# A two-layer transformer kernel: the order inside one step of layer 1's attention loop

## The chip, the core and the metric

The kernel runs on one core of a Trainium2 chip, in one launch. The metric is the device time of that core in microseconds, from the start of the execution to its end. A core has five engines that each work through a queue of their own, in order, and wait for one another by semaphores: TensorE (PE, matrix products and transposes), VectorE (DVE), ScalarE (ACT), GpSimd (POOL) and SyncE (SP, which issues DMAs here).

## The reference

The input `x` holds 2 sequences of 2048 tokens with 512 features (4096 tokens), the context 2 times 128 tokens. Four blocks follow one another, each added to `x`. All of it is float32.

```python
x = x + L0_xattn(layernorm(x), ctx, ...)   # 16 heads of 64, rope, tanh cap, causal
x = x + L0_ffn(layernorm(x), ...)          # fake-quantised gate, up, down; inner width 1408
x = x + L1_xattn(layernorm(x), ctx, ...)   # 16 heads of 32, masked
x = x + L1_ffn(layernorm(x), ...)          # one of 8 experts by argmax

def L1_xattn(q, k, v, mask, ...):
    Q = split_heads(q @ Wq.T + bq);  K = ...;  V = ...
    scores = where(mask, 1e-9, Q @ K.T / sqrt(32))
    return (softmax(scores) @ V) @ Wo.T + bo

def L1_ffn(x, Wg, bg, We, be):
    probs = softmax(x @ Wg + bg)              # 512 logits a token
    idx, p = argmax(probs), max(probs)
    return relu(x @ We[idx % 8] + be[idx % 8]) * p
```

## The kernel before

Tokens are worked on in 32 tiles of 128 tokens (`NT` = 32); `xs[n]` is the running `x` of tile `n` and stays on the chip. Layer 0's attention and feed-forward come first and take up to some 929 us of the span. Then comes the loop that the change is in, `for n in range(NT)`, whose step `n` does the attention of tile `n` and, behind it by one and two tiles, the rest of layer 1 for tiles `n - 1` and `n - 2`. Experts follow.

From that loop on the order of PE, DVE, ACT and POOL is the order in which the program is written, with no scheduler between (`manual_schedule`). So each engine's queue in a step is what the calls below issue, one after another:

- `biased(n - 1)`: POOL adds the output's bias to `xs[n - 1]` (L949).
- `normed(m)`: variance and reciprocal root for a tile five ahead (L92 to L101). The function that it returns centers that tile (DVE, `xn1`, L821) and, from tile 6 on, starts its transpose by DMA. In the steps 2 to 26 there is one such tile; these returned functions are the list `firsts`.
- `scores(n)`: 32 small products on PE into `sc` (L892). Then DVE masks half of the heads (L900) and takes their maxima (L905), and the other half likewise.
- `exponentials(n)`: 16 activations on ACT (L914); those of the second half leave their sums too.
- `queries(blk + 1, fs)`: the queries of the next block of 256 tokens. A step makes two of the four feature groups, one by `fs[:1]` and one by `fs[1:]`, each with 4 products on PE (8 instructions of 256 columns, L872) and an activation that puts the result into `qT` (L875).
- `shares(n, half)`: DVE takes the reciprocal of the half's sums (L922), POOL multiplies the half's 128x1024 exponentials by it (L923). For half 0 DVE has also to take the sums (L920).
- `logits(n - 2)`: PE, 4 products of 512 columns (L978) into `pl`. `picked(n - 2)`: DVE's largest logit and its index (L984, L988). `gated(n - 2)`: an activation over `pl` (L996) and small DVE instructions.
- `projected(n - 1)`: PE, the attention's output times `Wo` (L955) into `pw`, and the residual: DVE adds `pw` to `xs[n - 1]` (L956).
- `normed2(n - 1)`: statistics of the new `xs[n - 1]` (L92, L94, L963, L100), POOL's reciprocal root (L101). The function that it returns centers the tile (DVE, `xn2`, L821).
- `turned(n)`: PE transposes the shares, four tiles `pt` of four transposes each (L116); ACT copies each back (L931). The first two `pt` are of half 0, the others of half 1.
- `turned2(n - 1)`: PE transposes `xn2` (L116), ACT copies it (L972).
- `mixed(n)`: PE multiplies shares and values into `po` (L941), ACT copies that to `oT` (L946).

All of PE's results but the scores go through a pool `psm` of four banks. Both centerings come from one function, whose two wide operands, the tile and the scale spread over its columns, lie in SBUF:

```python
def center_by(dst, x, mean, r):
    nc.vector.scalar_tensor_tensor(dst, x, mean, r.to_broadcast([P, D]), ALU.subtract, ALU.mult)
```

The steps 24 to 29 carry a first part of the experts' routing on DVE as well; the steps 30 and 31 have no queries, but an expert each.

Of the kernel before, what the change touches and what calls it, by code (L numbers as in the profile page):

```python
# [18 lines left out]
AF = mybir.ActivationFunctionType  # L19
ALU = mybir.AluOpType  # L20
# [4 lines left out]
P = 128  # L25
B, S, T, D = 2, 2048, 128, 512
ND = D // P
NT = B * S // P
# [5 lines left out]
H1, DH1 = 16, 32  # L34
# [29 lines left out]
def two_layers(ctx: ExitStack, tc: tile.TileContext, a, out):  # L64
    nc = tc.nc
# [85 lines left out]
    with ExitStack() as l0:  # L151
# [231 lines left out]
        def queries(u, par):  # L383

            k, g = divmod(u, NG)
            j, b = blocks[k]
            if par == 0:
                if j not in tabs:
                    tables_in(j)
                ropes[u] = [mid.tile([P, B0], F32, name=f"rt{i}", bufs=1) for i in range(4)]  # L390
            pq, rt = psm.tile([P, B0], F32, name="pq", tag="m"), ropes[u]
            for c in range(ND):
                nc.tensor.matmul(  # L393
                    pq, wqs[c // 2][:, c % 2, par, g * P : (g + 1) * P], xnTs[k][:, c, :], start=(c == 0), stop=(c == ND - 1)
                )
            cos, sin = tabs[j]
            if par == 0:
                nc.vector.tensor_tensor(rt[0], pq, cos, ALU.mult)  # L398
                nc.vector.tensor_tensor(rt[1], pq, sin, ALU.mult)
                return  # L400
            qs[u] = [mid.tile([P, B0], F32, name=f"q{i}") for i in range(2)]
            nc.vector.tensor_tensor(rt[2], pq, sin, ALU.mult)  # L402
            nc.gpsimd.tensor_tensor(qs[u][0], rt[0], rt[2], ALU.subtract)  # L403
            nc.vector.tensor_tensor(rt[3], pq, cos, ALU.mult)
            nc.gpsimd.tensor_tensor(qs[u][1], rt[3], rt[1], ALU.add)
# [38 lines left out]
        def projected(u, t):  # L444

            k, g = divmod(u, NG)
            if g == 0:
                pws[k, t] = psq.tile([P, D], F32, name="pw", tag="pw", bufs=NB0)
            pw = pws[k, t]
            for f in range(2):  # L450
                nc.tensor.matmul(  # L451
                    pw, atts[u][:, f, t * P : (t + 1) * P], wo[:, 2 * g + f, :],
                    start=(g == 0 and f == 0), stop=(g == NG - 1 and f == 1),
                )
# [182 lines left out]
    with ExitStack() as up:  # L637
# [137 lines left out]
        rest = values(0)  # L775
# [86 lines left out]
        else:  # L862
            nc.scalar.copy(dst, transposed(psm, xn1s[n]))

    def queries(blk, fs):

        if blk not in qTs:
            qTs[blk] = mid.tile([P, ND, B1], F32, name="qT1")
        for f in fs:
            pq = psm.tile([P, B1], F32, name="pq", tag="m")  # L870
            for c in range(ND):
                nc.tensor.matmul(  # L872
                    pq, wq1[:, c, f * P : (f + 1) * P], xTs[blk][:, c, :], start=(c == 0), stop=(c == ND - 1)
                )
            nc.scalar.activation(  # L875
                qTs[blk][:, f, :], pq, AF.Identity, bias=bq[:, f : f + 1], scale=1.0 / math.sqrt(DH1)
            )

    def kept_keys(n):

# [35 lines left out]
    def shares(n, half):  # L916

        s, sm = ss_[n][half][0], sums[n][:, 8 * half : 8 * half + 8]
        if half == 0:
            nc.vector.tensor_reduce(sm, s, AX.X, ALU.add)  # L920
        rs = small.tile([P, 8], F32, name="rs")
        nc.vector.reciprocal(rs, sm)  # L922
        nc.gpsimd.tensor_tensor(s, s, rs.unsqueeze(2).to_broadcast([P, 8, T]), ALU.mult)  # L923
# [27 lines left out]
    def projected(n):  # L951

        pw = psm.tile([P, D], F32, name="pw1", tag="m")
        for c in range(ND):
            nc.tensor.matmul(pw, os_[n][:, c, :], wo1[:, c, :], start=(c == 0), stop=(c == ND - 1))  # L955
        nc.vector.tensor_tensor(xs[n], xs[n], pw, ALU.add)  # L956

    xn2, xn2T, pls, picks = {}, {}, {}, {}

    def normed2(n):  # L960

        mv = variance(xs[n])
        nc.vector.tensor_copy(xw[n][:, D : D + 1], mv[:, 0:1])  # L963
        r = xw[n][:, D + 1 : D + 2]
        rsqrt_eps(r, mv[:, 1:2])
        xn2[n] = mid.tile([P, D], F32, name="xn2", bufs=1)
        return lambda: center_by(xn2[n], xs[n], mv[:, 0:1], r)
# [6 lines left out]
    def logits(n):  # L974

        pl = pls[n] = psm.tile([P, D], F32, name="pl", tag="m")
        for c in range(ND):
            nc.tensor.matmul(pl, xn2T[n][:, c, :], wgate[:, c, :], start=(c == 0), stop=(c == ND - 1))  # L978
# [12 lines left out]
    def gated(n):  # L991

        negm, i8 = picks[n]
        pe = small.tile([P, 1], F32, name="pe1")

        nc.scalar.activation(  # L996
            scs[min(n + 2, NT - 1)][:, 0].rearrange("p c k -> p (c k)"), pls[n], AF.Exp, bias=negm, accum_out=pe
        )
        ei = small.tile([P, 1], U32, name="ei")
        nc.vector.tensor_scalar(ei, i8[:, 0:1], NE - 1, None, ALU.bitwise_and)  # L1000
        ef = small.tile([P, 1], F32, name="ef")
        nc.vector.tensor_copy(ef, ei)
        nc.vector.tensor_scalar(hot[:, n, :], iota_e, ef, None, ALU.is_equal)
        nc.gpsimd.tensor_tensor(cum[:, n + 1, :], cum[:, n, :], hot[:, n, :], ALU.add)
        nc.vector.memset(xw[n][:, D + 3 : D + 4], 0.0)

        def rest():
            nc.vector.reciprocal(xw[n][:, D + 2 : D + 3], pe)
            nc.sync.dma_start(out=x_dram[n * P : (n + 1) * P, :], in_=xw[n])

        return rest
# [224 lines left out]
    for n in range(NT):  # L1236
        blk, t = n // NB1, n % NB1
        ahead = blk + 1 < nblk
        fs = range(t * ND // NB1, (t + 1) * ND // NB1)
        if n > 0:  # L1240
            biased(n - 1)
        firsts = [m for m in (n + 2 * NB1, n + 2 * NB1 + 1) if m < NT and (m >= TURNED) == (m > n + 2 * NB1)]
        firsts = [normed(m) for m in firsts]
        scores(n)
        if 4 <= n < 4 + 2 * NE and n % 2 == 0:

            nc.scalar.dma_start(out=rowadd, in_=v_dram[(n - 4) // 2].partition_broadcast(P))

        late = t == 0 and n > 1
        if ahead and not late:  # L1250
            queries(blk + 1, fs[:1])
        if late:
            logits(n - 2)
        exponentials(n)
        if ahead and late:
            queries(blk + 1, fs[:1])
        if n == 0:
            for i in range(NT - held, NT - held + 2):
                down(i)
                widened(i + 2)  # L1260
        shares(n, 0)
        if n > 1:
            if not late:
                logits(n - 2)
            picked(n - 2)
        shares(n, 1)
        if n > 0:
            projected(n - 1)
            normed2(n - 1)()
        firsts = [first() for first in firsts]  # L1270
        rest = gated(n - 2) if n > 1 else None
        if n + 1 < NT:
            kept_keys(n + 1)
        for first in firsts:
            if first:
                first()
        if 0 < n <= NE:
            load(we[:, n - 1], a["L1_ffn_We"][n - 1].rearrange("(c p) f -> p c f", p=P))
        if ahead:
            queries(blk + 1, fs[1:])  # L1280
        if n == 0:
            for i in range(NT - held + 2, NT):
                down(i)
            dwn.close()
            ffd.close()
            moe = ctx.enter_context(tc.tile_pool(name="moe", bufs=1, side="right"))
            we = moe.tile([P, NE, ND, D], F32, name="we")
        if 4 <= n < 4 + 2 * NE:
            e, half = divmod(n - 4, 2)
            for c in range(2 * half, 2 * half + 2):  # L1290
                nc.gpsimd.tensor_tensor(we[:, e, c, :], we[:, e, c, :], rowadd, ALU.add)
        if not ahead:

            expert(n - NT + NB1)
        turned(n)
        if rest:
            rest()
        if n > 0:
            turned2(n - 1)
        mixed(n)  # L1300
        if t == NB1 - 1 and blk + 2 < nblk:
            for t in range(NB1):
                turned1((blk + 2) * NB1 + t)
        if n == NTA + 2:
            route = routing(True)
        if route:
            for _ in range({NTA + 2: 4, NTA + 3: 1}.get(n, 2)):
                if next(route, route) is route:
                    route = None
                    for j in range(4):  # L1310
                        gathered(j)
                    break
        if n == NT - NB1 - 1:
            for j in range(3):
                centered_x(j)
            turned_x2(0)
    biased(NT - 1)
    projected(NT - 1)
    normed2(NT - 1)()
    logits(NT - 2)  # L1320
    picked(NT - 2)
# [54 lines left out]
```

## Time and profile before

| | |
|---|---|
| median of 3 runs | 1600.61 us (1597.93 to 1601.00) |
| profiled execution: its time, its span | 1599.43 us, 1597.4 us |
| TensorE clock granted, mean | 0.995 |
| busy: PE, DVE, ACT, POOL | 1551.3, 1192.5, 720.4, 586.8 us |
| loop: first scores of step 0, of step 31 | 928.9, 1416.1 us |
| a step between 2 and 23 | 15.32 us (337.1 us for 22) |

The span runs from the first to the last instruction; the execution's own time is 2.0 us more. PE's busy time is the sum of its instructions' times, which overlap their neighbours'. In the timeline a row is one instruction or several equal ones: start, time, engine, line, operation, and in brackets how long the engine had sat idle and what released it. Where PE's rows are concerned, an instruction's end is modelled, and the next may start before it.

### The profile page before, as it was taken

What the parts mean: (1) busy time and instruction counts of PE and PEld (TensorE: products, weight loads), DVE (VectorE), ACT (ScalarE), POOL (GpSimd) and SP (SyncE); (2) the same over time, 40 slices, a digit from 0 to 9 for tenths busy, and PEclk for the clock granted to TensorE, in tenths of its full rate; (3) what the DMA queues carried; (4) which work ended last, traced back from release to release, by engine and by line L of the source; (5) the groups of instructions that cost most, each with busy time, mean ns of one, the idle gap of its engine ahead of it and who ended that gap; (6) DMA issues with size and microseconds to landing.
All of it is one profiled execution on the core that took longest, in us unless ns stands there. A gap on an engine that the chain in (4) does not pass through costs nothing. (4 is left out here: it accounts for less than half of the span.)

```text
span 1597.4 us, 26167 instructions
## 1 busy us (share of the span) xinstructions
PE 1551.3 (97%) x9542; PEld 909.1 (57%) x9542; DVE 1192.5 (75%) x2333; ACT 720.4 (45%) x1537; POOL 586.8 (37%) x580
## 2 busy tenths in 40 slices
PE   7999999999999999999999999999999999999997
PEld 5655555555555555544444466666666666654443
DVE  3467777777777886589986678888888888877442
ACT  1222222222222222243335566777777776763442
POOL 2232222222222222110005654555565444544553
PEclk9999999999999999999999999999999999999999
DMA  9511212111111220367768734221311111114553
GB/s 321 188 37 41 47 40 47 40 47 40 51 46 41 59 60 1 117 169 205 179 173 278 271 132 143 48 47 34 55 45 36 41 28 41 41 47 131 162 162 89
DMA packets 180571, 150.90 MB, mean 94 GB/s; under 512 B 97089, under 2 KB 144665, under 8 KB 180444
## 3 DMA queue, kind: packets, MB, share of 16 engines
q1 hardware_dynamic: 170188, 127.25, 28.5%
q0 software_dynamic: 6240, 18.70, 3.8%
q10 hardware_dynamic: 4016, 3.29, 0.9%
q8 instruction: 76, 1.25, 0.3%
q14 instruction: 51, 0.42, 0.1%
HBM read 89.97 MB, written 41.79 MB: 82 GB/s over the span
## 5 line engine op out<-in xcount | busy, mean ns | idle before, releaser
L419 ACT ACTIVATE pr<-sc 128x1024 f32<-128x1024 f32 x64 | 65.6, 1024 | 421.6 <-PE sc L414 421.4
L393 PE MATMUL pq<-xnT,wq 128*128 128x256 f32 x1024 | 254.4, 391 | 0.0
L451 PE MATMUL pw<-wo,att 128*128 128x512 f32 x512 | 230.8, 593 | 0.0
L393 PEld LDWEIGHTS pq<-xnT,wq 128*128 128x128 f32 x1024 | 184.4, 189 | 67.1 <-issue 44.0
L914 ACT ACTIVATE s<-s,mx 128x128 f32<-128x128 f32 x512 | 175.3, 388 | 28.1 <-DVE mx L905 28.1
L923 POOL TENSOR_TENSOR s<-s,rs 128x1024 f32<-128x1024 f32 x64 | 120.9, 1903 | 149.6 <-DVE rs L922 149.1
L403 POOL TENSOR_TENSOR q<-rt,rt 128x256 f32<-128x256 f32 x64 | 46.7, 730 | 339.7 <-DVE rt L402 335.2
L451 PEld LDWEIGHTS pw<-wo,att 128*128 128x128 f32 x512 | 96.9, 190 | 96.4 <-issue 89.9
L441 DVE RECIPROCAL rd<-sc 128x256 f32<-128x256 f32 x64 | 112.4, 1757 | 46.5 <-PE sc L435 46.5
L1195 PE MATMUL pz<-we,x 128*128 x312 | 139.3, 598 | 1.8 <-ACT x L832 1.6
L872 PE MATMUL pq<-xT,wq 128*128 128x256 f32 x512 | 122.6, 382 | 0.0
L978 PE MATMUL pl<-wgate,xnT 128*128 128x512 f32 x256 | 116.7, 599 | 0.0
L955 PE MATMUL pw<-wo,oT 128*128 128x512 f32 x256 | 115.2, 592 | 0.7 <-ACT oT L946 0.7
L872 PEld LDWEIGHTS pq<-xT,wq 128*128 128x128 f32 x512 | 96.0, 190 | 33.1 <-issue 20.3
L398 DVE TENSOR_TENSOR rt<-pq,rope_cos 128x256 f32<-128x256 f32 x64 | 27.0, 422 | 104.2 <-PE pq L393 104.2
L749 ACT ACTIVATE gate<-pg,gsc 128x512 f32<-128x512 f32 x88 | 60.5, 687 | 93.9 <-PE pg L744 84.0
L1195 PEld LDWEIGHTS pz<-we,x 128*128 128x128 f32 x312 | 58.2, 192 | 68.4 <-issue 65.2
L92 DVE BATCH_NORM_STATS2 st<-x 128x6 f32<-128x512 f32 x130 | 89.4, 688 | 6.0 <-DMA x<-in_ctx 3.8
L744 PE MATMUL pu<-xqT,wuT 128*128 128x512 bf16 x352 | 90.3, 379 | 2.6 <-DVE h L752 2.4
L744 PE MATMUL pg<-xqT,wgT 128*128 128x512 bf16 x352 | 90.3, 379 | 0.0
L900 DVE SCALAR_TENSOR_TENSOR s<-sc,keep 128x1024 f32<-128x1024 f32 x64 | 78.1, 1220 | 14.3 <-PE sc L892 9.1
L955 PEld LDWEIGHTS pw<-wo,oT 128*128 128x128 f32 x256 | 48.6, 190 | 55.3 <-issue 53.6
(226 smaller groups left out, 2811.8 us busy)
## 6 DMA issues: line engine op xcount, KB each, us to landing
h_dram<-h SPq DMA_DIRECT2D x88, 256.0 KB
hq<-h_dram SPq DMA_DIRECT2D x31, 704.0 KB
x_dram<-x SPq DMA_DIRECT2D x32, 258.0 KB
x<-in_x SPq DMA_DIRECT2D x32, 256.0 KB
we<-in_L_ffn_We SPq DMA_DIRECT2D x8, 1024.0 KB
xnT<-in_x_turned SPq DMA_DIRECT2D x14, 512.0 KB
along<-stat_dram SPq DMA_DIRECT2D x14, 256.0 KB
w_in<-in_L_ffn_w_gate SPq DMA_DIRECT2D x11, 256.0 KB
```

What stands on the lines that cost most here:

```text
L92: nc.vector.bn_stats(out=st, in_=x)
L393: nc.tensor.matmul(pq, wqs[c // 2][:, c % 2, par, g * P : (g + 1) * P], xnTs[k][:, c, :], start=(c == 0), stop=(c == ND - 1))
L441: nc.vector.reciprocal(rd, sc[:, 0, B0:])
L451: nc.tensor.matmul(pw, atts[u][:, f, t * P : (t + 1) * P], wo[:, 2 * g + f, :], start=(g == 0 and f == 0), stop=(g == NG - 1 and f == 1),)
L744: nc.tensor.matmul(dst, w[:, c, i * P : (i + 1) * P], xqTs[blk][:, c, :], start=(c == 0), stop=(c == ND - 1),)
L872: nc.tensor.matmul(pq, wq1[:, c, f * P : (f + 1) * P], xTs[blk][:, c, :], start=(c == 0), stop=(c == ND - 1))
L900: nc.vector.scalar_tensor_tensor(s, sc[:, 2 * half : 2 * half + 2].rearrange("p r c k -> p (r c) k"), -MASKED, keeps[n].unsqueeze(1).to_br ...
L914: nc.scalar.activation(s[:, h, :], s[:, h, :], AF.Exp, bias=mx[:, h : h + 1], **accum)
L923: nc.gpsimd.tensor_tensor(s, s, rs.unsqueeze(2).to_broadcast([P, 8, T]), ALU.mult)
L955: nc.tensor.matmul(pw, os_[n][:, c, :], wo1[:, c, :], start=(c == 0), stop=(c == ND - 1))
L978: nc.tensor.matmul(pl, xn2T[n][:, c, :], wgate[:, c, :], start=(c == 0), stop=(c == ND - 1))
L1195: nc.tensor.matmul(pz, ring[j][:, c, :], we[:, bass.ds(e, 1), c, :], start=(c == 0), stop=(c == ND - 1))
```

## The change

All of it is in the order within a step. On PE the projection of tile `n - 1` now comes first behind the scores, then the logits of tile `n - 2`, then the first group of queries, and of the second group three of its four products; the fourth comes behind the transposes of the shares. Before, the first group of queries stood ahead of the logits in odd steps and behind them in even ones, and the projection behind both.

On DVE the residual's addition now stands between the two halves of the shares, ahead of `picked`; the reciprocal of half 1 follows these. The centering of the tile five ahead (`xn1`) now stands ahead of the centering of tile `n - 1` (`xn2`); it stood behind it.

On ACT the activation of the first group of queries comes behind the exponentials in all steps, and that of the second group behind the four copies of the shares. The queues of POOL and SP keep their order.

```diff
-    def queries(blk, fs):
+    def queries(blk, fs, held=0):
...
+            products(range(ND - held))
+            if held:
+                return lambda: products(range(ND - held, ND)), rest
+            rest()
...
-        nc.vector.tensor_tensor(xs[n], xs[n], pw, ALU.add)
+        return lambda: nc.vector.tensor_tensor(xs[n], xs[n], pw, ALU.add)
...
-        late = t == 0 and n > 1
-        if ahead and not late:
-            queries(blk + 1, fs[:1])
-        if late:
+        residual = projected(n - 1) if n > 0 else None
+        if n > 1:
             logits(n - 2)
         exponentials(n)
-        if ahead and late:
+        if ahead:
             queries(blk + 1, fs[:1])
...
         shares(n, 0)
+        if residual:
+            residual()
         if n > 1:
-            if not late:
-                logits(n - 2)
             picked(n - 2)
         shares(n, 1)
-        if n > 0:
-            projected(n - 1)
-            normed2(n - 1)()
+        second = normed2(n - 1) if n > 0 else None
+
         firsts = [first() for first in firsts]
+        if second:
+            second()
         rest = gated(n - 2) if n > 1 else None
...
-        if ahead:
-            queries(blk + 1, fs[1:])
+
+        end = queries(blk + 1, fs[1:], 1) if ahead else ()
...
         turned(n)
+        for part_ in end:
+            part_()
         if rest:
             rest()
         if n > 0:
             turned2(n - 1)
         mixed(n)
...
-    projected(NT - 1)
+    projected(NT - 1)()
```

Built, a step has four banks for these tiles in turn: `pw`, `pl` and the two `pq`. The second `pq` keeps its bank over the transposes, so the four `pt` take the banks of `pw`, of the first `pq`, of `pl`, and then again that of the first `pt`.

More of the change, by code (lines that the diff above doesn't have):

```diff
@@ L870, in queries, with products, rest @@
             pq = psm.tile([P, B1], F32, name="pq", tag="m")
-            for c in range(ND):
-                nc.tensor.matmul(
-                    pq, wq1[:, c, f * P : (f + 1) * P], xTs[blk][:, c, :], start=(c == 0), stop=(c == ND - 1)
-                )
-            nc.scalar.activation(
-                qTs[blk][:, f, :], pq, AF.Identity, bias=bq[:, f : f + 1], scale=1.0 / math.sqrt(DH1)
-            )
+            def products(cs, f=f, pq=pq):
+                for c in cs:
+                    nc.tensor.matmul(
+                        pq, wq1[:, c, f * P : (f + 1) * P], xTs[blk][:, c, :], start=(c == 0), stop=(c == ND - 1)
+                    )
+            def rest(f=f, pq=pq):
+                nc.scalar.activation(
+                    qTs[blk][:, f, :], pq, AF.Identity, bias=bq[:, f : f + 1], scale=1.0 / math.sqrt(DH1)
+                )
+            products(range(ND - held))
+            if held:
+                return lambda: products(range(ND - held, ND)), rest
+            rest()
     def kept_keys(n):
```

## The prediction

> **What bounds the kernel now.** First the page's busy times: PE is busy nearly throughout, so only PE's waits can be won.
>
> ```profile
> PE 1551.3 (97%) x9542; PEld 909.1 (57%) x9542; DVE 1192.5 (75%) x2333; ACT 720.4 (45%) x1537; POOL 586.8 (37%) x580
> ```
>
> Next, busy times by stretch, for steps 2 to 23: 337.1 us, 15.32 us each.
>
> ```profile
> 965.30:1302.40 337.10, 335.02 (x2557) 223.26 (x2556) 289.45 (x614) 252.88 (x769) 185.42 (x163) 1.00 0.21 47
> ```
>
> Then the timeline of one step; its scores start at 1072.51. Below, every time counts from there.
>
> ```profile
> 1080.15 0.20 DVE L922 RECIPROCAL rs<-sums 128x8 f32<-128x8 f32 x1
> 1080.27 0.65 DVE L984 MAX8 m<-pl 128x8 f32<-128x512 f32 x1
> 1080.52 3.76 POOL L923 TENSOR_TENSOR s<-s,rs 128x1024 f32<-128x1024 f32 x2 [3.77 <-DVE rs L922]
> 1081.09 0.69 DVE L988 FIND_INDEX8 i<-m,pl 128x8 uint32<-128x512 f32 x1
> 1082.01 0.20 DVE L922 RECIPROCAL rs<-sums 128x8 f32<-128x8 f32 x1 [0.23 <-ACT s L914]
> 1082.31 1.89 PE L872 MATMUL pq<-xT,wq 128*128 128x256 f32 x8
> 1082.59 0.69 DVE L956 TENSOR_TENSOR x<-x,pw 128x512 f32<-128x512 f32 x1 [0.37 <-PE pw L955]
> 1083.31 0.70 DVE L92 BATCH_NORM_STATS2 st<-x 128x6 f32<-128x512 f32 x1
> 1084.04 1.91 PE L116 MATMUL pt<-ident,s 128*128 128x128 f32 x16
> 1084.33 0.14 DVE L100 TENSOR_SCALAR ve<-mv 128x1 f32<-128x1 f32 x1
> 1084.55 0.55 POOL L101 TENSOR_TENSOR x<-ve,minus_half 128x1 f32<-128x1 f32 x1 [0.27 <-DVE ve L100]
> 1085.13 0.75 DVE L821 SCALAR_TENSOR_TENSOR xn<-x,mv 128x512 f32<-128x512 f32 x1 [0.66 <-POOL x L101]
> 1085.80 0.74 DVE L821 SCALAR_TENSOR_TENSOR xn<-x,mv,r 128x512 f32<-128x512 f32 x1
> 1086.03 0.63 PE L116 MATMUL pt<-ident,xn 128*128 128x128 f32 x4
> 1086.59 1.31 PE L941 MATMUL po<-s,v 128*32 128x128 f32 x32
> 1087.83 1.17 PE L892 MATMUL sc<-kT,qT 32*128 32x128 f32 x32
> ```
>
> PE transposes the shares from 11.53; sixteen at 0.11 us let it go on at 13.28. The transposes of xn2 start at 13.52, 0.15 after their centering ends (13.37): PE loses about 0.24 a step there, all that a better order can win. The other chain ends near it: POOL's two multiplications run back to back, 1.90 each, from 8.01 to 11.77, and PE wants half 1 at 12.40. That is 0.63 of slack.
>
> Last, the timeline where DVE meets POOL, in steps 1 and 0 and just before the loop:
>
> ```profile
> 959.25 1.27 POOL L949 TENSOR_TENSOR x<-x,bob 128x512 f32<-128x512 f32 x1
> 959.32 1.75 DVE L821 SCALAR_TENSOR_TENSOR xn<-x,mv 128x512 f32<-128x512 f32 x1 [0.85 <-POOL x L101]
> ```
>
> ```profile
> 939.97 4.10 POOL L923 TENSOR_TENSOR s<-s,rs 128x1024 f32<-128x1024 f32 x2 [0.45 <-ACT qT L875]
> 940.37 1.92 DVE L882 TENSOR_SCALAR keep<-masks 128x128 f32<-128x128 uint8 x1
> ```
>
> ```profile
> 925.03 0.88 DVE L804 CAST hb<-hi 128x1408 bf16<-128x1408 int8 x1
> 925.19 1.13 POOL L101 TENSOR_TENSOR r<-ve,minus_half 128x1 f32<-128x1 f32 x1 [0.23 <-DVE ve L100]
> ```
>
> A centering takes 0.75; issued under POOL's addition it took 1.75 and ended 0.55 after it (961.07 against 960.52). The mask took 1.92 under L923, 0.22 elsewhere. POOL's root takes 0.55; under a DVE cast it took 1.13 and ended 0.41 after it. So these instructions shut each other out.
>
> **The change part by part, in a step from 2 to 23.** *Scores to the first reciprocal:* unchanged, so half 0's stands at 7.64. *Projection first:* it needs oT, which ACT copies from 0.11 to 0.70 (1072.62, 0.59 long); the scores hold PE until 1.1. Nothing is paid; 0.4 covers it, and a later oT would cost its excess. *Residual sooner:* pw is ready by 5, so DVE adds behind the reciprocal: 7.76 (0.12 later, as MAX8 is now). That lengthens DVE's queue ahead of half 1 by 0.72 (1082.59 to 1083.31): MAX8 8.48, index 9.30 (0.82 later), the reciprocal 10.02. Today it waits for ACT until 9.50, so 0.52 of the 0.72 shows. POOL starts 0.37 after a reciprocal: half 1 runs 10.39 to 12.29, not 11.77.
>
> *PE up to half 1:* the same products in another order, less a quarter of the second queries (a quarter of 1.73 is 0.43): transposes start at 11.10, and half 1 is wanted at 11.97. It comes at 12.34 (in step 1 PE started 0.05 after POOL's end: 958.78, 958.83). A new wait of 0.37. Behind it stand PE's eight transposes (0.9) and the held product (0.43): PE is free for xn2 at about 13.70. The held product fills the old 0.24 hole, but later than the hole was.
>
> *The centering of the tile ahead, now first:* statistics follow the reciprocal, ve at 11.16 (10.14 plus 1.02, as 1083.31 to 1084.33), so this centering is issued at about 11.3, in the middle of POOL's half 1. Today both centerings run while POOL is idle. By the row of step 1 it ends 0.55 after POOL: 12.84. POOL's root for xn2, queued behind half 1, meets that centering as the row before the loop met the cast: done 0.41 after it, 13.25. xn2 then runs 13.28 to 14.03, and PE's transposes start 0.15 later, 14.18: another wait of 0.48. From there 0.56 to po and 1.24 to the next scores, as now: 15.98. The step grows by 0.66; 22 of them by **14.5**.
>
> The Trainium skill speaks to this ("SBUF — State Buffer", Who interferes with whom): a DVE instruction with two SBUF inputs and a GpSimd instruction that reads SBUF lock each other out, and the second to issue waits for the first's end. Taken to the letter the centering would run whole after POOL (13.04), the root whole after that, and the step would grow by 1.0, 22 of them by 22, as an estimate. The rows above have durations (0.55 and 0.41 instead of 0.75 and 0.55), so I take 0.66.
>
> *ACT and banks:* the first queries' activation now follows the exponentials: pq ends near 9.9, so it runs to 10.4, the gating to 11.1; the transposes that need those banks start at 11.5 and 12.34. The fourth pt reuses the first's bank: copied by 12.3, wanted at 12.8. The second activation, behind the copies, ends by 14.6; the next scores need it after 16. All nothing; the least cover is 0.5.
>
> *The other steps.* Step 0: PE waits for half 1 anyway, so the held product adds its 0.43: 0.4. Step 1 has two tiles to center ahead of xn2, and POOL's bias addition can lock out xn2 in turn: between a gain of 0.9 (no lock) and a loss of 1.5; by the row at 959.32 xn2 ends some 0.6 later than now, so 0.7. Steps 24 to 29: step 24's growth is swallowed, since step 25's scores wait for routing on DVE; the end of 25 moves by 1.0 (0.52 and the lock's 0.46), 26 adds 0.3, 27 to 29 have no tile ahead and add 0.2 each: 1.9, between 0.5 and 4. Steps 30 and 31: transposes stand at 11.95 behind the expert, xn2 comes 0.05 late: 0.1. The tail keeps its order.
>
> Sum: 0.4 + 0.7 + 14.5 + 1.9 + 0.1 = 17.6. On the profiled execution's own 1599.43 (span 1597.4 and 2.0 around it) that makes 1617.0; the median of the runs lies 1.2 above that execution.
>
> **Rivals.** *No lock (11%):* if the centering runs under POOL undisturbed, it ends at 12.05, root 12.80, xn2 13.58, PE 13.73: 0.21 a step, 4.6 in 22. Step 1 gains 0.9, the others 0.4, 1.2 and 0.1: 1604.8. It would be much the same if the centering waits but the root slips in ahead of it (xn2 behind the centering, 13.57). For it: statistics (L92) run beside L923 unhindered now. Against: the three meetings above.
>
> *The hole closes, faster (6%):* half 1's multiplication ends by 11.8, so PE never waits and 0.25 a step goes: 5.5, some 0.6 in later steps: about 1593.5. It decides at half 1's reciprocal: it must start by 9.55 instead of my 10.02. For it: the reciprocal has 0.23 of idle time ahead of it now. Against: the addition is 0.69, and the queue's order is fixed.
>
> *The clock drops (5%):* around step 1 the stretch 961 to 966 has a granted clock of 0.66, behind waits of 1.72, 0.77 and 1.20. My new waits, 0.37 and 0.48 in 16 us, are smaller than the 0.84 and 0.46 of step 27, where the clock stays 1.00. If it dropped in every step, 3.4 us at half clock would cost up to 1.7 each: up to 1655. The Trainium skill ("TensorE: Matmul & The Clock Gate", HAM oscillation) warns of idle gaps above some 3.4 us; by it step 1 should not have dropped at all, so here the rows decide.
>
> That the change does not do what it says is excluded by the built order of the queues.
>
> **How the numbers follow.** My case holds 74%; 4% lies between cases. Its own range: upward 2.1 and 0.8 by the upper bounds of steps 24 to 29 and of step 1, and 3.1 if the root waits its whole 0.55 behind the centering (0.14 in 22 steps), 1623; downward 1.4 and 2.2 by the lower bounds and 2.2 for 0.1 a step, 1611. A range of 1604 to 1624 takes in "no lock" too and leaves out about 14%. A measurement of this kernel tells about 0.2% (3.2 us) from no change: faster 0.07, same 0.03, slower 0.90.
>
> **What would show it.** In the changed profile: steps of 15.98; half 1's reciprocal at 10.0; the centering with r as long as 1.5 instead of 0.74; the root L101 near 1.0 instead of 0.55; PE waiting about 0.4 for POOL's shares and 0.5 for xn2 in every step. I am wrong on the lock if the centering stays 0.74 and the step is 15.53; wrong on the queue if PE has no wait for the shares.

## The result, and the profile after

The changed kernel is slower: median 1608.85 us of 6 runs (1605.14 to 1610.08) against 1599.27 of 6 runs of the kernel before (1597.64 to 1601.09); the ratio is 1.0054, with a 95% interval of 1.0043 to 1.0065. The profiled execution took 1609.41 us, its span 1607.4. So the direction was right and the size was about half of the 17.6 us forecast; the time lies inside the range, below my own case's 1611 to 1623.

The page's busy times have hardly moved, which says that no engine got more to do:

```profile
PE 1552.7 (97%) x9519; PEld 903.3 (56%) x9542; DVE 1206.7 (75%) x2333; ACT 723.2 (45%) x1537; POOL 599.0 (37%) x580
```

DVE's and POOL's extra 14 and 12 us are mostly time in which they block each other. The busy times by stretch for steps 2 to 23 (start and end, length, then PE, PEld, DVE, ACT, POOL) give 340.81 us, or 15.49 a step. The same stretch of before was 337.07. So a step grew by 0.17 and not by 0.66:

```profile
966.77:1307.58 340.81, 334.30 (x2553) 217.68 (x2552) 303.27 (x614) 255.54 (x769) 195.36 (x163) 1.00 0.21 47
```

The timeline of one step shows how. Its scores start at 1075.20; the times in the text count from there.

```profile
1082.82 0.20 DVE L931 RECIPROCAL rs<-sums 128x8 f32<-128x8 f32 x1
1082.94 0.65 DVE L965 TENSOR_TENSOR x<-x,pw 128x512 f32<-128x512 f32 x1
...
1083.51 0.69 DVE L993 MAX8 m<-pl 128x8 f32<-128x512 f32 x1
...
1084.37 0.69 DVE L997 FIND_INDEX8 i<-m,pl 128x8 uint32<-128x512 f32 x1
1084.98 0.18 DVE L931 RECIPROCAL rs<-sums 128x8 f32<-128x8 f32 x1
...
1085.33 1.90 POOL L932 TENSOR_TENSOR s<-s,rs 128x1024 f32<-128x1024 f32 x1 [0.24 <-DVE rs L931]
...
1086.11 1.68 DVE L821 SCALAR_TENSOR_TENSOR xn<-x,mv,r 128x512 f32<-128x512 f32 x1
1086.29 2.09 PE L116 MATMUL pt<-ident,s 128*128 128x128 f32 x16
...
1087.19 1.00 POOL L101 TENSOR_TENSOR x<-ve,minus_half 128x1 f32<-128x1 f32 x1
...
1088.22 0.75 DVE L821 SCALAR_TENSOR_TENSOR xn<-x,mv 128x512 f32<-128x512 f32 x1 [0.44 <-POOL x L101]
...
1089.12 0.63 PE L116 MATMUL pt<-ident,xn 128*128 128x128 f32 x4 [0.30 <-DVE ei L1009]
...
1089.68 1.08 PE L950 MATMUL po<-s,v 128*32 128x128 f32 x32
...
1090.69 0.39 PE L901 MATMUL sc<-kT,qT 32*128 32x128 f32 x4
```

Read it from POOL's row. Half 1 runs 10.13 to 12.03. The centering with `r` (xn1) is issued at 10.91 in its middle and takes 1.68 instead of 0.74: it ends at 12.59, 0.56 after POOL. The root takes 1.00 instead of 0.55 and ends 0.40 after the centering. Then xn2 at 13.02, PE's transposes of it at 13.92 (13.52 before), `po` 0.56 later. (The bracket in the transposes' row names a small DVE instruction that ran meanwhile; what they read is xn2.) This is the forecast's chain, link by link. But it starts 0.24 sooner than forecast (half 1's reciprocal at 9.78, not 10.02), and at its end 1.01 us lie from `po` to the next scores, not 1.24.

All profiles taken of the two kernels, four of before and three of after, give the whole sum. Each row is the mean, of step 1 the lowest and the highest; the differences add up to 7.9, which is also the difference of the mean times of these profiled executions.

| us | before | after | difference |
|---|---|---|---|
| up to the scores of step 0 | 929.0 | 929.3 | +0.3 |
| step 0 | 18.05 | 18.02 | 0.0 |
| step 1 | 16.75 to 18.32 | 17.42 to 18.79 | +0.4 |
| steps 2 to 23 | 337.08 | 340.82 | +3.75 |
| steps 24 to 30 | 113.72 | 113.95 | +0.2 |
| scores of step 31 to the end | 182.0 | 185.3 | +3.3 |

Step 1 is the one row that has to be cleaned of the clock: two profiles of before have a stretch at half clock in it (18.32, 18.26) and two have none (16.76, 16.75); of after, one profile has a long one there, of 6.8 us (18.79). The other two of after have one of 3.4 us in it that costs nothing: two later runs with none there take as long, 17.41 (the pause filled, with the same order in this step) and 17.42 (no held product). So without the clock step 1 grew from 16.75 to 17.42, by 0.67.

### The profile page after: what moved, and what is told of

Its sections match the earlier page's. It is cut to its first block, busy times and chain, and to the rows that moved or that the text cites. A ratio compares the mean times of both kernels' runs of the same rounds, so it can differ in the third digit from the quotient of the medians.

```text
span 1607.4 us, 26160 instructions
## 1 busy us (share of the span) xinstructions
PE 1552.7 (97%) x9519; PEld 903.3 (56%) x9542; DVE 1206.7 (75%) x2333; ACT 723.2 (45%) x1537; POOL 599.0 (37%) x580
## 5 line engine op out<-in xcount | busy, mean ns | idle before, releaser
L964 PE MATMUL pw<-wo,oT 128*128 128x512 f32 x256 | 120.1, 612 | 2.3 <-issue 2.3
L987 PEld LDWEIGHTS pl<-wgate,xnT 128*128 128x128 f32 x256 | 48.6, 190 | 61.2 <-issue 61.2
```

## The experiments

**The changed kernel again**, without an edit.

> The changed kernel once more, unchanged. In its first profile the regular steps 2 to 23 took 15.49 us each (15.32 before), 22 x 0.17 = 3.8 us in all; another 5 us lay outside them: 1.0 ahead of the loop, and 4.4 behind it, where ScalarE stood for 1.6 us ahead of a copy between the first two experts and a stretch of 3.4 us at half clock followed. Theory 'by chance': the two stretches at half clock and the copy's delay do not come again at the same place; the steps stay 15.49, loop +4.6, and the 4.4 behind the loop are gone: about 1604 to 1605 for an execution like that. Rival 'by the order': the delay at step 31's copy comes again and the time is about 1609 in profile and rounds.

Measured: 1608.85 us, ratio 1.005 (1.0032 to 1.0068); steps of 15.49; 186.4 us behind the scores of step 31. "By chance" fell: the stretch at half clock and the delay at step 31 came again at the same place. My expectation also blamed the wrong engine. ScalarE's copy was idle because TensorE's signal for the end of `po` came only then (1439.20 in the first profile's semaphore events, 1.9 us after the last product had started).

**xn2 first**: only the order of the centerings is undone.

```diff
-        second = normed2(n - 1) if n > 0 else None
+        if n > 0:
+            normed2(n - 1)()
         firsts = [first() for first in firsts]
-        if second:
-            second()
```

> The changed kernel with the two centerings in their old order: xn2 ahead of xn1, all else as changed. Theory 'lock': the root for xn2 runs straight behind POOL's half 1 (12.0 to 12.55 from the scores), xn2 12.58 to 13.33, PE's transposes of it at about 13.5, where the held product already fills up to 13.45; a step takes about 15.05, 0.44 less than changed and 0.27 less than before, over some 25 steps -10 us: 1594 to 1599, faster than both. Rival 'queue': what the step lost comes from the later half 1 alone (POOL 10.13 to 12.04); then the step stays at about 15.5 and the time at 1609.

Measured: 1597.78 us, ratio 0.998 (0.997 to 0.999); most steps 15.05, 331.6 us for steps 2 to 23. Its timeline, in a step that starts at 1070.60:

```profile
1080.74 1.90 POOL L932 TENSOR_TENSOR s<-s,rs 128x1024 f32<-128x1024 f32 x1 [0.24 <-DVE rs L931]
1082.60 0.55 POOL L101 TENSOR_TENSOR x<-ve,minus_half 128x1 f32<-128x1 f32 x1
1083.18 0.75 DVE L821 SCALAR_TENSOR_TENSOR xn<-x,mv 128x512 f32<-128x512 f32 x1 [1.59 <-POOL x L101]
1083.85 0.74 DVE L821 SCALAR_TENSOR_TENSOR xn<-x,mv,r 128x512 f32<-128x512 f32 x1
```

Half 1 stands where it stands in the changed kernel (10.14 to 12.04), but nothing meets: root 0.55, both centerings 0.75 and 0.74. The whole loss of the step, and more, goes with this one edit: 0.44 a step. Against the kernel before, run beside it (1601.08), the time falls by 3.3 us and not by the 5.5 that steps 2 to 23 win; the 3 us behind step 31 stay.

**The exchange alone**, in the kernel before.

```diff
-            normed2(n - 1)()
+        second = normed2(n - 1) if n > 0 else None
         firsts = [first() for first in firsts]
+        if second:
+            second()
```

> The kernel before with nothing but the two centerings exchanged: xn1 ahead of xn2. Theory 'lock': xn1's centering is issued near POOL's end of half 1 and the root for xn2 meets it, so the root takes up to 1.0 instead of 0.55 and ends at about 13.06, xn2 13.09 to 13.84, PE's transposes of it at 13.99 instead of 13.52; with 1.0 to 1.2 from po to the next scores a step takes 15.56 to 15.8, +0.24 to +0.48, about +5 to +11 us: 1605 to 1611. Rival 'no lock': the root slips in beside the centering, or xn2 follows the centering without loss; xn2 at most 0.2 later, step 15.32 to 15.5, at most +4 us.

Measured: 1607.18 us, ratio 1.004 (1.0025 to 1.0055); steps of 15.52, +0.21.

```profile
1085.36 0.74 DVE L821 SCALAR_TENSOR_TENSOR xn<-x,mv,r 128x512 f32<-128x512 f32 x1
1085.52 0.99 POOL L101 TENSOR_TENSOR x<-ve,minus_half 128x1 f32<-128x1 f32 x1 [0.27 <-DVE ve L100]
```

Here half 1 has ended (11.77 in a step from 1073.49) when the centering is issued (11.87), so the centering is undisturbed and the root alone is shut out. It ends 0.41 after the centering, as the row just before the loop (0.41 behind the cast) had let expect. So a root that meets the centering is enough to cost 0.2 a step.

**The held product alone**, in the kernel before: the fourth product of the second queries, and its activation, behind `turned(n)`, as in the change.

> The kernel before with nothing but the fourth product of the second queries held back behind the shares' transposes. Theory 'copies': in the kernel before, the products behind po waited for ScalarE's last copies of the shares, which is why 1.24 us lie from po to the next scores and only 1.01 after the change; with PE's transposes of the shares 0.43 earlier and the copies too, po no longer waits: xn2 stays the limit at 13.5, po to scores 1.0, a step 15.1, -0.2, in 22 steps -5 us: about 1595. Rival 'fixed': the 1.24 stays as xn2's hole only becomes the held product, and the step stays at 15.32, the time within 2 us of before.

Measured: 1597.30 us, ratio 0.9973 (0.9962 to 0.9984); steps of 15.085, -0.23. This part of the change pays, by itself. What it wins is read from ScalarE's copies of the shares (L931, L940) against `po`. Before, and below it the held product alone:

```profile
1084.73 2.05 ACT L931 COPY s<-pt 128x512 f32<-128x512 f32 x4
...
1086.59 1.31 PE L941 MATMUL po<-s,v 128*32 128x128 f32 x32
```

```profile
1082.56 2.05 ACT L940 COPY s<-pt 128x512 f32<-128x512 f32 x4 [1.66 <-POOL s L932]
...
1084.85 1.08 PE L950 MATMUL po<-s,v 128*32 128x128 f32 x32
```

Before, the copies end at 1086.78, 0.19 after `po` has started, and the products that need the last of them wait; with the product held the copies end at 1084.61, 0.24 ahead of it. xn2 and `po` start when they did before (12.62 and 14.07 into the step); only the distance from `po` to the next scores falls, from 1.24 to 1.01. It is 1.01 too in the changed kernel and in the exchange alone, whose `po` comes later.

**No held product**, all else as changed.

```diff
-        end = queries(blk + 1, fs[1:], 1) if ahead else ()
+        end = ()
+        if ahead:
+            queries(blk + 1, fs[1:])
```

> The changed kernel with all four products of the second queries ahead of the shares' transposes again, as before the change; all else as changed. Theory 'xn2 sets the step': the transposes start at 11.53, find half 1 there (12.04 against 12.40 wanted), and end at 13.27; xn2 comes at 13.92 as in the changed kernel, po 14.48, next scores 1.01 later: the step stays 15.49, the time about 1609. Rival 'the held product fills a hole that would cost': the copies come later and po waits for them again, 1.24 instead of 1.01: 15.72, +0.23 a step, about 1614.

Measured: 1608.00 us, ratio 1.005 (1.0033 to 1.0067); steps of 15.49. In the changed kernel the held product is worth nothing: xn2 is the limit, `po` is late, and the copies have time either way.

**The residual late**: in the changed kernel, `residual()` behind `shares(n, 1)`.

> The changed kernel with the residual's addition back behind half 1's reciprocal, all else as changed. Theory 'queue and lock': half 1's reciprocal comes at 9.50 (9.78 changed), POOL's half 1 runs 9.87 to 11.77; the centering is issued near 11.35 under it and ends 0.55 after it, 12.32; the root ends 0.40 after that, 12.72; xn2 12.75 to 13.50, PE's transposes at 13.65, and a step takes 15.22 (15.49 changed): over 24 steps -6.5 us, about 1602. Rival 'the lock alone sets the step': the later addition makes the centering later by what POOL gains; the step stays within 0.05 of 15.49, about 1609.

Measured: 1603.54 us, ratio 1.0023 (1.0013 to 1.0034), steps of 15.46. The expected 15.22 did not come, and the row that says why was new to me:

```profile
1079.34 0.20 DVE L931 RECIPROCAL rs<-sums 128x8 f32<-128x8 f32 x1
1079.99 0.70 DVE L993 MAX8 m<-pl 128x8 f32<-128x512 f32 x1 [0.45 <-PE pl L987]
...
1081.47 0.18 DVE L931 RECIPROCAL rs<-sums 128x8 f32<-128x8 f32 x1
```

MAX8 now waits for the logits. With the projection ahead of them on TensorE their last product starts 7.64 after the scores, and MAX8 cannot start before 8.28, so half 1's reciprocal comes at 9.76 without the addition and at 9.78 with it. The addition fills a wait that another part of the change had made. (The time fell by 5 us although the step lost only 0.03; against the mean of after's profiles 1.3 lie ahead of the loop, 1.1 in steps 24 to 30 and 0.8 behind step 31, and no run takes these apart.)

**The logits first**: as in the last run, and `logits(n - 2)` ahead of `projected(n - 1)`.

```diff
-        residual = projected(n - 1) if n > 0 else None
         if n > 1:
             logits(n - 2)
+        residual = projected(n - 1) if n > 0 else None
```

> As the run with the residual late, and on TensorE the logits of tile n - 2 ahead of the projection of tile n - 1 again; centerings still xn1 first, product still held. Theory 'logits': in the changed kernel and with the residual late the last logits product starts 7.64 from the scores, so MAX8 cannot start before 8.28 and half 1's reciprocal not before 9.76, addition or not; with the logits first MAX8 starts at 7.76, the reciprocal at 9.50, POOL's half 1 runs 9.87 to 11.77, the centering is issued near 11.35 and ends 0.55 after POOL, 12.32; root to 12.72, xn2 12.75 to 13.50, PE's transposes 13.65, the step 15.22: over 22 steps -5.3 us against the run with the residual late. Rival 'ScalarE': the reciprocal waits at 9.76 for something of ScalarE's queue that the change moved there; then it stays 9.76 and the step 15.46.

Measured: 1600.59 us, ratio 1.000 (0.9991 to 1.001); steps of 15.22 as expected. In a step from 1070.95:

```profile
1080.45 0.20 DVE L931 RECIPROCAL rs<-sums 128x8 f32<-128x8 f32 x1 [0.24 <-ACT s L923]
1080.57 0.65 DVE L965 TENSOR_TENSOR x<-x,pw 128x512 f32<-128x512 f32 x1
1082.33 0.94 DVE L821 SCALAR_TENSOR_TENSOR xn<-x,mv,r 128x512 f32<-128x512 f32 x1
1082.68 1.00 POOL L101 TENSOR_TENSOR x<-ve,minus_half 128x1 f32<-128x1 f32 x1
```

The reciprocal is back at 9.50, POOL's half 1 at 9.87 to 11.77, the centering ends at 12.32 and the root at 12.73. So "projection first" cost 0.24 a step, by way of the logits.

**Half 1 in two instructions**, on POOL, in the changed kernel; DVE's order is as changed.

```diff
-        nc.gpsimd.tensor_tensor(s, s, rs.unsqueeze(2).to_broadcast([P, 8, T]), ALU.mult)
+        for hs in (slice(0, 4), slice(4, 8)) if half else (slice(0, 8),):
+            nc.gpsimd.tensor_tensor(
+                s[:, hs], s[:, hs], rs[:, hs].unsqueeze(2).to_broadcast([P, hs.stop - hs.start, T]), ALU.mult
+            )
```

> The changed kernel with POOL's multiplication of half 1 in two instructions of 512 columns. Theory 'lock by the instruction': the centering issued at 10.91 waits for the first of them alone (10.13 to 11.09) and ends 0.55 after it, near 11.65, so it takes about 0.75; the second multiplication is locked out meanwhile and ends near 12.45, the root runs 12.45 to 13.0 undisturbed, xn2 to 13.8 and the step stays near 15.5. Rival 'lock until POOL pauses': the centering runs 10.91 to 12.6 again, and the root about 1.0, the step again 15.5. The centering's duration tells them apart, not the time.

Measured, in a single run: 1610.40 us, steps of 15.60.

```profile
1084.65 2.49 POOL L933 TENSOR_TENSOR s<-s,rs 128x512 f32<-128x512 f32 x2 [0.21 <-DVE rs L931]
1085.45 0.79 DVE L821 SCALAR_TENSOR_TENSOR xn<-x,mv,r 128x512 f32<-128x512 f32 x1
1087.10 0.54 POOL L101 TENSOR_TENSOR x<-ve,minus_half 128x1 f32<-128x1 f32 x1
```

The centering slips in between the two: issued at 10.91, it ends at 11.70, 0.55 after POOL's first half (11.15). The second half, locked out in turn, ends at 12.60. So the lock holds for an instruction, not for a burst; splitting moves the wait to the other engine and loses 0.1.

**Before three times more, and after a third time**, for the stretch behind step 31.

> The kernel before, unchanged. What is open: about half of the 8 us between the two kernels lies outside the loop. From the scores of step 31 to the end of the span the kernel before took 181.3 us in its one profile; the changed kernel (twice) and three others with the same order there took 184.9 to 186.4. Theory 'chance of one profile': the kernel before shows 185 too when it is profiled again, with the 3 us stall between the first two experts and a stretch at half clock near it; then the loop alone (+3.0 to +4.6) is the change's doing and its median should come out near 1604, not 1600. Rival 'of the program': it is 181 again and the time 1600 to 1601; then something that differs by the program as built, not by the order of that stretch, costs the others 4 us there.

> The kernel before once more, for its stretch behind the loop. Two profiles had 181.3 and 182.5 us from the scores of step 31 to the end of the span, eight others of changed orders 183.5 to 186.4, all of these with a stretch at half clock between the first two experts. By chance of the execution: one in two of these repeats shows that stretch and 184 or more. As a property of the program: 181 to 183 again, without that stretch.

> The same as the run before it: by chance of the execution 184 or more in one of the two, as a property of the program 181 to 183 in both.

> The changed kernel a third time, for the same stretch: as a property of the program 185 to 186.5 with the stretch at half clock between the first two experts; by chance of the execution it may be missing and the stretch then takes about 183.5. The regular step is 15.49 in either case.

Measured: before 1600.51 us (median of 10 runs), 1600.09 and 1599.36, with 182.5, 182.0 and 182.3 us behind the scores of step 31; after 1603.62, with 183.7. So it is not the chance of one profile, though the first profile of before was lucky in one thing: TensorE's pause between `po` and `pw` of step 31, from the start of the last product to that of the next, is 2.2 us in the other three and was 0.95 there. (The product itself takes 0.27 of it; the rest is idle.) In after it is 2.5 to 2.6, and a stretch at half clock follows in all three profiles, in before in none. The busy times by stretch show it for the first profile of after (third from last stands the granted clock):

```profile
1436.90:1440.30 3.40, 1.11 (x26) 0.69 (x18) 0.52 (x2) 0.95 (x2) 2.89 (x3) 1.00 0.44 134
1440.30:1443.70 3.40, 3.40 (x5) 1.33 (x4) 0.00 (x0) 0.00 (x0) 0.61 (x1) 0.50 0.25 99
```

All changes of the clock within a profile's span are whole multiples of 3.413 us apart. Laid on that grid, the pause has at least 1.9 us of idle PE inside one window in each of the nine profiles (of any kernel up to here) in which the next window is at half clock. In the four where the next stays at full clock and the pause is 2.2, the grid cuts it, with at most 1.73 in one window. Two of the nine are the exchange alone and the held product alone, whose order behind step 31 and whose pause (2.2) are those of before; so the order there does not decide by itself. For before, in its fourth profile, with TensorE's rows (`issue`: the profile shows nothing that it waited for):

```profile
1428.60:1432.00 3.40, 2.34 (x39) 1.44 (x37) 1.75 (x8) 1.81 (x4) 1.96 (x3) 1.00 0.20 76
1432.00:1435.40 3.40, 2.53 (x6) 1.25 (x7) 0.00 (x0) 0.58 (x1) 1.90 (x2) 1.00 0.51 157
1435.40:1438.80 3.40, 3.40 (x9) 1.52 (x8) 1.78 (x5) 0.00 (x0) 0.16 (x1) 1.00 0.00 0
```

```profile
1429.47 1.47 PE L941 MATMUL po<-s,v 128*32 128x128 f32 x32
1432.87 3.70 PE L955 MATMUL pw<-wo,oT 128*128 128x512 f32 x8 [1.93 <-issue]
```

**The pause filled**: in the changed kernel, behind the loop, the logits of tile 30 ahead of the projection of tile 31.

```diff
     biased(NT - 1)
+    logits(NT - 2)
     projected(NT - 1)()
     normed2(NT - 1)()
-    logits(NT - 2)
```

> The changed kernel with one thing moved behind the loop: the logits of tile 30 ahead of the projection of tile 31 on TensorE, so that ready work stands in the pause behind step 31. Theory 'the pause makes the drop': TensorE goes on within 0.3 us of its last product instead of 2.5, no stretch at half clock follows there, and from the scores of step 31 to the products of expert 2 it takes about 23.2 us instead of 27.25; the stretch from step 31 to the end 181 to 182.5 instead of 183.7 to 186.4, the time about 1605 against 1608.9. Rival 'the clock drops anyway' (by the time since the last one, or the power drawn): a stretch at half clock stands near 1437 to 1441 again, TensorE has 1.7 us more there and the time falls by 2 at most.

Measured: 1605.28 us, ratio 1.0041 (1.0026 to 1.0055). The TensorE timelines, of after and of this run:

```profile
1436.46 1.10 PE L950 MATMUL po<-s,v 128*32 128x128 f32 x32
1439.86 5.40 PE L964 MATMUL pw<-wo,oT 128*128 128x512 f32 x8 [2.29 <-issue]
1445.09 3.60 PE L987 MATMUL pl<-wgate,xnT 128*128 128x512 f32 x8
```

```profile
1433.91 1.66 PE L950 MATMUL po<-s,v 128*32 128x128 f32 x32
1435.50 3.70 PE L987 MATMUL pl<-wgate,xnT 128*128 128x512 f32 x8
1439.04 3.60 PE L964 MATMUL pw<-wo,oT 128*128 128x512 f32 x8
...
1448.46 0.66 PE L116 MATMUL pt<-ident,x 128*128 128x128 f32 x4 [1.52 <-ACT sc L1005]
```

No pause, and no stretch at half clock there; the signal for `po` comes 0.29 us after the last product has started, not 1.9: `pw` takes 3.60 again instead of 5.40, and expert 2 starts 23.2 us after the scores of step 31 instead of 27.3. So the pause made the drop. But 2.1 of the 4 us are given back behind expert 2, where TensorE now waits 1.52 us for ScalarE's `sc` (L1005), and another stretch at half clock came at 1486.6. From step 31 to the end it is 183.9 us, not the 181 to 182.5 expected. The time is the 1605 expected, but only in part by the move: the kernel before, run beside it, is 2.2 us faster here too (1598.92 against 1601.08 beside the changed kernel's repeat). Against it the growth went from 7.8 to 6.4, so the move brought some 1.4 us, as much as the stretch behind step 31 fell (185.3 to 183.9).

**Two versions to beat both**: the same move behind the loop, on xn2 first and on the held product alone.

> The changed kernel with xn2 centered first, and the same move behind the loop. Theory: as xn2 first, 15.05 a step, and behind the loop about 4 us less: 1593.5 to 1595. Rival 'the clock drops anyway': 1596 to 1598.

> The kernel before with the held product alone, and the same move behind the loop. Theory: 15.09 a step, and behind the loop 3.5 to 4 us less: 1593 to 1594.5. Rival 'the clock drops anyway': 1595.5 to 1597.5.

Measured: 1596.30 us, ratio 0.9987 (0.9978 to 0.9995), and 1597.27 us, ratio 0.9991 (0.9982 to 1.0001). Both missed the times expected (1593.5 to 1595, and 1593 to 1594.5). Beside the kernel before on the same chip (1598.92) the move behind the loop shows no gain over what the two orders had without it (0.998 and 0.9973). The pause and the drop behind it are gone in both, but a stretch at half clock has come at 1476.9 and 1476.4, as at 1486.6 in the last run: each time 67 us behind the scores of step 31. From there to the end it is 182.9 and 184.8 us (185.2 and 185.4 without the move). The lowest ratio remains that of the held product alone, though the intervals of the other three overlap with it.

## Why the prediction was right or wrong, step by step

What failed is the sum for one step: +0.66 was forecast and +0.17 came, 3.75 us in 22 steps instead of 14.5. The lock, its main mechanism, was right. Two steps of the prediction failed in it. "Residual sooner" put half 1's reciprocal 0.24 too late, and nearly all of the delay that did come has its cause in "Projection first", at which "nothing is paid". And the 1.24 from `po` to the next scores "as now" was 1.01. Outside these steps two errors ran against each other: steps 24 to 31 grew by 0.2 instead of 2.0, and the stretch behind step 31, put at nothing, grew by 3.3. That the time came as near the forecast as it did is in part luck: without these 3.3, which have another cause, it would be some 1605.5 (an estimate, 1608.85 less 3.3).

- **The lock: right, and it is the cause of what the steps lose.** Centering 0.55 behind POOL's end (forecast 0.55; the rounded row above gives 0.56), root 0.41 behind the centering (0.41), within 0.01 in every step from 2 to 23; with the order undone the step falls by 0.44 (xn2 first), with the order alone it rises by 0.21 (the exchange alone). On the order the Trainium skill ("SBUF — State Buffer", Who interferes with whom) says that whichever of the two issues first has the shared ports for its whole instruction while the other is blocked. Read to the letter, the other would then run its own whole length. The rows say that it ends 0.55 after, though alone it takes 0.75, and the measurement decides: that reading would have put the step 0.34 higher.
- **"Projection first: nothing is paid": wrong.** I checked what the projection needs (oT) and not what stands behind it. It moved the end of the logits' products from 4.80 and 6.53 (in turn, as the first queries stood behind or ahead of them) to 8.24, behind the time at which DVE wants them (7.75). Logits first is 0.24 a step better.
- **"Residual sooner", 0.52 at half 1's reciprocal: mis-sized, 0.28 measured.** I took 0.72 from the addition's start to that of the statistics behind it. But these need its result; MAX8 does not, and starts 0.57 after the addition, at 8.31. It is 0.55 later than before and the reciprocal 0.28, so the reciprocal's slack was 0.27, not 0.20. As it stands, the 0.28 is not even the addition's: the late logits alone make 0.26. Two parts of the change ran into the same wait; I had seen one of them, and charged it nearly double.
- **PE's wait for half 1, 0.37: 0.12**, by the same 0.24 (from the eighth transpose of the shares to the ninth 0.23 us, 0.11 before).
- **"Then 0.56 to po and 1.24 to the next scores, as now": wrong by 0.23.** The 1.24 held a wait of `po` for ScalarE's copies. A later `po` does not have it. Carried over as a fixed duration, it put 5 us into the sum. With this term and that of half 1's reciprocal put right the forecast step of 15.98 becomes 15.98 - 0.24 - 0.23 = 15.51; 15.49 was measured. Nor was the 0.24 ahead of xn2's transposes "all that a better order can win": xn2 first takes 0.27 off the step of before.
- **Step 1, 0.7: right** (0.67, without the clock). Step 0, 0.4: nothing came. Steps 24 to 31, 2.0: 0.2 for 24 to 30 (113.72 and 113.95 in the table). By the profiles' means steps 24 and 25 grew by 0.2 and 1.2, but 26 to 29 fell by 1.1 together, where growth was forecast; no run shows why. In the range, step 1's lower bound was taken at 2.2 below the 0.7; its own gain of 0.9 makes that 1.6, and 1611.8 instead of 1611.2.
- **"The tail keeps its order", at nothing: wrong by about 3.** TensorE's order behind step 31 is the same, but its pause there is 0.35 longer and lay in one window of the clock's grid in all three profiles, which costs 1.7 (`pw` 5.40 instead of 3.70). Some 0.9 more behind the start of expert 2 and the 0.3 ahead of the loop are within what profiles of one kernel differ by.
- **The rivals.** No lock is excluded by the rows. The hole did not close here, though one part of the edit wins what that rival described: the held product alone, at -5 us in the steps. It wins it behind `po`, not by an earlier half 1. The clock did not drop inside the steps (1.00 for 2 to 23).

What stays open: why TensorE's signal for `po` of step 31 comes 1.5 to 1.9 us late wherever that pause shows, and not in the first profile of before (0.29). It is 0.29 too in the three runs that have ready products behind `po`, so no run shows it late where TensorE can go on at once. Open is also whether the kernel before falls on the good side of the clock's grid every time by its own timing or had luck four times.

## What to carry to other kernels

Before two instructions of VectorE with wide operands in SBUF are exchanged, write down what GpSimd runs at that time, small instructions too (the root is 128x1): the same two centerings cost 0.4 us a step in one order and nothing in the other. When a product is moved ahead on TensorE, price what it pushes back, down to the engine that wants it next. And take start-to-start times from a pair whose second does not wait for the first, or the wait is charged twice.

## What the hardware showed that I had not expected

- The granted clock halves for 3.413 us after a window of the same length in which TensorE was idle for about half of it; no pause of the whole length is needed. Over 17 profiles, from 60 us on and up to the end of the experts, every window with 2.1 us idle or more was followed by half clock and none with under 1.5 was, but for two behind a drop that had already begun; between them both occur. The Trainium skill ("TensorE: Matmul & The Clock Gate") tells of such a free-running window, under What's actually happening, and warns, under HAM oscillation, of idle gaps above some 3.4 us. The first agrees with the 3.413 here; the second is too mild, since the pauses of 2.2 to 2.6 us behind step 31 cost 1.7 each in nine profiles (`pw` 5.38 to 5.40 instead of 3.70).
- The lock between VectorE and GpSimd goes instruction by instruction and changes hands between two instructions of one engine that follow each other without a pause (0.79 for the centering, 1.49 for the second half of POOL's work in the split run).
